# A four-layer graph network on one core: two sections of 64x64 products per pair, a tied norm in layer 3, and factors turned by chunks

## Chip, cores and metric

The kernel runs on one core of a Trainium2 chip, in one launch. The metric is the device time of that execution in microseconds (us). The host only lays the inputs out (the adjacency both ways round, some weights transposed).

The engines are named as in the profile: PE is TensorE (matrix products, with PEld its loading of the stationary operand), DVE is VectorE, ACT is ScalarE, POOL is GpSimd and SP is SyncE, which starts most transfers here. Each works through its own queue in order and waits for the others at semaphores.

## The reference

128 graphs of 64 nodes with 512 features, fp32, go through four layers. Every layer is `x = x + layer(relu(layernorm(x)), adj)`. Cut to what matters:

```python
# layer 0: a gate per node, softmax over the 64 nodes of a graph
q, k = split(h @ Wqk);  v = h @ Wv
agg = einsum('bij,bjd->bid', adj, k * mask)
w   = mask * einsum('bid,bid->bi', q, agg) / sqrt(512)
out = softmax(w, axis=1)[:, :, None] * v
# layer 1: one head, exp weights times adjacency
weight = adj * exp(einsum('bqd,bkd->bqk', h @ Wq.T + bq, h @ Wk.T + bk))
out = einsum('bqk,bkd->bqd', weight / weight.sum(2), h @ Wv.T + bv)
# layer 2: eight heads of 64, scores times adjacency, softmax, projection Wo
# layer 3: alpha = adj * exp(leaky_relu(sj + si + ab)), rows normalized to a transition
H = 0; Xk = h
for k in range(3):
    H = H + Xk @ Wk[k] + bk[k];  Xk = einsum('bij,bjd->bid', transition, Xk)
out = relu(H)
```

## The kernel before

**Blocks, pairs and steps.** A block is 256 tokens, that is four graphs, held as two tiles of 128 partitions (two graphs each). There are 32 blocks. Layers 0 and 1 run together, in pairs of blocks: for blocks 2p and 2p+1 the four steps are layer 0 of the even block, layer 0 of the odd one, layer 1 of the even one, layer 1 of the odd one (list `steps`). Their result goes to DRAM (`x1`); then layer 2 runs over all blocks, storing to `x2`, and layer 3 over all blocks.

**Products of 512x512.** The 256x512 by 512x512 products are made by a scheme of seven half-size products (class `Product`, L230). A product has two PSUM tiles, `ab_*` and `dc_*`, and runs as `first`, `second` and `late`; between them VectorE and ScalarE take intermediate values (`u_*`, L288, and `p_*`, L287 and L296) that free the accumulators for the late products. GpSimd forms four sums of the transposed input (`sums`, tiles S). The sums of the weights are formed once. `side_by_side` (L354) runs two products together and calls lists of `between` actions at three points: after the first product's `first`, and ahead of each `late`.

**Norms.** `norm` (L165) takes statistics on VectorE (`stats`, `mv`, `ve`), the root on GpSimd (`rstd`), a product on VectorE (`nmr`), and applies both with the relu on ScalarE (tiles `h`). `transposed` (L190) turns `h` on TensorE through PSUM tiles `tr`. `prepare(i + 1)` issues the next step's norm in the first `between` list of a step, `turned(i + 1)` its transposes in the last.

**Layer 0.** The neighbour sum `agg` is formed over `h` and multiplied by folded weights (Wq times Wk transposed: `fold`, slot `m0`), so that one product g and one product v are made per block. `am` is the adjacency times the mask column (GpSimd), `pa` (L400) the neighbour sums, one 64-wide product per graph into one half of a PSUM tile. ScalarE copies `pa` to `agg`; after the product g, VectorE makes the dots `w` and spreads them on a diagonal (`wd`). The rest (`layer0_end`, L572) runs in the next step's first `between` list: `sm_w` on TensorE, the softmax on VectorE and ScalarE, and x is updated.

**Layer 1.** Its products are again folded: g = h (Wq' Wk) and v. `products` (L378) makes the scores `sc` of a graph, 64 by 64 each, 32 matmuls with 128 rows by 64 columns of the array. `e` is their exp times the adjacency. `layer1_end` (L622) makes the row sums `den` and `po = e v`, one 64-wide product per graph; VectorE takes the reciprocals `r` (L636), adds `po r` to x (L638), and SyncE stores x.

**Where the 64-wide products stand.** All products that work on graphs (`sc`, `den`, `po`, `pa`) use parts of the array 64 wide; everything around them is 128 wide. `layer1_end` of block b is kept in `open_end`, which is called by the next step of an odd block. In a pair there are three places with such products: in the third step `sc` of the even block; in the fourth step the even block's end followed by `sc` of the odd block, after which the next pair's even `pa` comes; in the next pair's second step the odd block's end followed by that block's own `pa`. PSUM has eight banks: pool `ps_tr` two (transposes, `po`), `ps_mm` four (`ab_*` and `dc_*`, a `den` or `pa` at times), `ps_sc` two (scores, `pa`, row sums).

**Setup of layer 1.** `setup1` fetches Wq and Wk of layer 1, transposes both by `transpose_weights` (L419: sixteen 128x128 transposes per factor, into four PSUM tiles `tw_q` and four `tw_k`), and multiplies them in `folded` (`pf`, L450). The transposes go row chunk k by row chunk, each into every tile m. ScalarE copies all four `tw_q`; of the `tw_k` it copies those in `on_scalar`, VectorE the others, in the order of m.

**Layer 3.** For the first blocks, `layer3_norm` and `layer3_dots` run within layer 2's last steps. `layer3_dots` (L835) makes two dots per tile and the diagonal `di` (L848), from which TensorE makes `sm_i` (L408). A statement under `tc.issue_after(X)` is put behind instruction X in the order of issue; statements with no such tie are placed by a scheduler, which may put them ahead of what is written before them. A norm of layer 3 whose input has arrived can so stand earlier on VectorE than its place in the text.

Of the kernel before, what the change touches and what calls it, by code (L numbers as in the profile page):

```python
# [8 lines left out]
FP = mybir.dt.float32  # L9
# [4 lines left out]
P = 128  # L14
# [11 lines left out]
def kernel(ctx: ExitStack, tc: tile.TileContext, a: dict, out: bass.AP):  # L26
# [177 lines left out]
    def norm_T(x, name: str):  # L204
        hs = norm(x, name)
        return hs, transposed(hs, name)

    kept_ab, kept_p = [None], [None]
    behind = [None]

# [164 lines left out]
                act()  # L375
        return made

    def products(uT, vT, name: str):  # L378

        ps = ps_sc.tile([P, TT, N], FP, tag="sc", name=f"sc_{name}")  # L380
        for t in range(TT):
            for k in range(K):
                for g in range(2):
                    c = slice(t * P + g * N, t * P + (g + 1) * N)
                    nc.tensor.matmul(
                        ps[g * N : (g + 1) * N, t, :], uT[:, k, c], vT[:, k, c],
                        start=(k == 0), stop=(k == K - 1), skip_group_check=True,
                    )
        return ps
# [29 lines left out]
    def transpose_weights(*pairs):  # L419

        pts = [
            [
                pool.tile([P, K, P], FP, tag=tag, name=f"tw_{name}_{m}")
                for m, (pool, tag) in enumerate(places)
            ]
            for w, name, places, on_scalar, to in pairs
        ]
        for k in range(K):
            for (w, *_), mine in zip(pairs, pts):
                for m, pt in enumerate(mine):  # L430
                    nc.tensor.transpose(pt[:, k, :], w[k][:, m * P : (m + 1) * P], ident)
        last = [None, None]
        for m in range(K):
            for (_, _, _, on_scalar, to), mine in zip(pairs, pts):
                flat = mine[m].rearrange("p k i -> p (k i)")
                if m in on_scalar:
                    last[1] = nc.scalar.copy(to[m], flat)
                else:
                    last[0] = nc.vector.tensor_copy(to[m], flat)
        return last  # L440
# [29 lines left out]
    def setup1():  # L470


        qT, kT = (factor(a[f"L1_W{c}"], c, 1, nc.sync) for c in "qk")

        bias = big.tile([P, 2, P, K], FP, tag="v", name="b1qk")
        for i, n in enumerate(("L1_bq", "L1_bk")):
            nc.sync.dma_start(
                bias[:, i], a[n].rearrange("(o p) k -> o p k", o=1).to_broadcast([P, P, K])
            )
        w1v = fetched("L1_Wv", 3, nc.sync)  # L480
        yield

        rows = [med.tile([P, K, P], FP, tag="pT", name=f"b1_{i}", bufs=3) for i in range(2)]
        for i, r in enumerate(rows):
            nc.scalar.copy(r.rearrange("o k p -> o p k"), bias[:, i])
        rows = [r.rearrange("o k p -> o (k p)") for r in rows]
        yield
        u = const.tile([P, K], FP, tag="u1", name="u1")
        cc = small.tile([P, K], FP, tag="cc", name="c1", bufs=1)
        d = const.tile([P, 1], FP, tag="d1", name="d1")  # L490
        c1 = const.tile([P, 2, D + 1], FP, tag="u3", name="c1")[:, 0, :D]
        m = slot(2, "fold1")
        qt, kt = (
            f[K:] + [m[:, spare].rearrange("p k o -> p (k o)")]
            for f, spare in ((qT, T1), (kT, T2))
        )
        transpose_weights((qT, "q1", in_mm, range(K), qt))
        taken = transpose_weights((kT, "k1", elsewhere, (1, 3), kt))
        folded(kt, qt, 1, m, lambda: layer0_end(0, *softmax))
        formed(m, nc.gpsimd)  # L500
        with tc.issue_after(behind[0].ins):
            formed(w1v, nc.gpsimd)

        def dots(*sums):
            for to, x, by in sums:
                junk = med.tile([P, D], FP, tag="e2", name="bias1", bufs=3)
                nc.vector.scalar_tensor_tensor(
                    junk, x, 1.0, rows[by], ALU.mult, ALU.mult, accum_out=to
                )

        with tc.issue_after(taken[0].ins):
            dots((d, rows[0], 1))
            dots(*((u[:, k : k + 1], qT[k], 1) for k in range(K)))
            dots(*((cc[:, k : k + 1], kT[k], 0) for k in range(K)))

        crow = tc.dram_tile([1, D], FP, name="c1_row")
        nc.sync.dma_start(crow.rearrange("o (k p) -> p (o k)", p=P), cc)
        nc.sync.dma_start(c1, crow.to_broadcast([P, D]))
        w2 = [fetched(f"L2_W{c}", 4 + i, nc.sync) for i, c in enumerate("qk")]
        for w in w2:  # L520
            later(w)
        yield m, u, c1, d, w1v, w2


    def layer0(b: int, x, adjT, hs, hT, between, before):
        ops = sums(hT, f"0_{b}")
        gv = big.tile([P, 2, TT, D], FP, tag="qk", name=f"gv_{b}")
        am = small.tile([P, TT, N], FP, tag="am", name=f"am_{b}", bufs=2)
        with tc.issue_after(behind_norm[0][0].ins):
            nc.gpsimd.tensor_tensor(  # L530
# [2 lines left out]
                mcol[:, b * TT : (b + 1) * TT].unsqueeze(2).to_broadcast([P, TT, N]),  # L533
                ALU.mult,
            )
        before()
        pa = [
            pool.tile([P, D], FP, tag=tag, name=f"pa_{b}_{t}")
            for t, (pool, tag) in enumerate((
                ((ps_sc, "sc"), (ps_sc if b % 2 else ps_mm, "sc" if b % 2 else "mm"))  # L540
                if b else ((ps_tr, "tr"),) * 2
            ))
        ]
        aggs = [
            med.tile([P, D], FP, tag="agg", name=f"agg_{b}_{t}", bufs=2) for t in range(TT)
        ]
        for t, to, at in neighbour_sums(pa, am, hs):
            nc.scalar.copy(aggs[t][to], pa[t][at])

        parts = [  # L550
            (ops, m0, None, lambda p: p.store(gv[:, 0]), f"g0_{b}"),
# [43 lines left out]
    def layer1(b: int, x, adjT, hs, hT, between, before):  # L595
# [15 lines left out]
                    hc, hs[t], 1.0, c1, ALU.mult, ALU.mult, accum_out=be[:, t : t + 1]  # L611
                )
        nc.vector.tensor_scalar(be, be, d1, None, ALU.add)
        before()
        s = products(gT, hT, f"1_{b}")
        e = small.tile([P, TT, N], FP, tag="e", name=f"e1_{b}")
        for t in range(TT):
            nc.scalar.activation(e[:, t, :], s[:, t, :], AF.Exp, bias=be[:, t : t + 1])
        nc.vector.tensor_tensor(e, e, adjT, ALU.mult)
        return of_v, v, e  # L620

    def layer1_end(b: int, x, v, e, to):  # L622

        po = [ps_tr.tile([P, D], FP, tag="tr", name=f"po1_{b}_{t}") for t in range(TT)]
        pool, tag = (ps_mm, "mm") if b + 1 < n_blk else (ps_sc, "sc")
        den = [pool.tile([P, 1], FP, tag=tag, name=f"den1_{b}_{t}") for t in range(TT)]
        for t in range(TT):
            for g in range(2):
                nc.tensor.matmul(
# [5 lines left out]
        for t in range(TT):  # L635
            nc.vector.reciprocal(r[:, t : t + 1], den[t])  # L636
        for t, out_at, at in parts:
            nc.vector.scalar_tensor_tensor(  # L638
                x[out_at, t, :], po[t][at], r[at, t : t + 1], x[out_at, t, :], ALU.mult, ALU.add
            )  # L640
        nc.sync.dma_start(tokens(to), x)
# [189 lines left out]
    def layer3_norm(b: int):  # L831
        x, adjT = loaded3.pop(b)
        return x, adjT, norm(x, f"3_{b}")

    def layer3_dots(b: int, x, adjT, hs):  # L835


# [2 lines left out]
        for s in range(2):  # L840
# [4 lines left out]
                    accum_out=sij[:, s, t : t + 1],  # L845
                )
        di = small.tile([P, TT, N], FP, tag="e", name=f"di_{b}")
        nc.vector.tensor_tensor(  # L848
            di,
            eye.unsqueeze(1).to_broadcast([P, TT, N]),  # L850
            sij[:, 1, :].unsqueeze(2).to_broadcast([P, TT, N]),
# [128 lines left out]
    def prepare(i: int):  # L980
        layer, b = steps[i]
        if b not in loaded:
            loaded[b] = load_x(b, x_d[rows(b), :], 0), load_adjT(b, 0)
        normed[i] = norm(loaded[b][0], f"{layer}_{b}")

    def second():
        with tc.issue_after(of_m0.ins):
# [12 lines left out]
    def fetch2(b: int):  # L1000
        if b < n_blk:
            loaded2[b] = load_x(b, x1[b], 2), load_adjq(b)
# [28 lines left out]
    next(setup)  # L1031
    begun = []

    def nothing():
        pass

    open_end = nothing
    for i, (layer, b) in enumerate(steps):
        if i == len(steps) - 2:
            fetch2(0)  # L1040
# [7 lines left out]
            between[n].append(end)  # L1048
        begun = []
        if i + 1 < len(steps):  # L1050
            between[0].append(lambda: prepare(i + 1) if i else second())
            between[2].append(lambda: turned(i + 1))
        else:
            fetch2(1)
            between[0].append(lambda: first2(0, of_v))
            between[2].append(lambda: turned2(0))
        if layer == 0:
            softmax = layer0(b, *loaded[b], *normed[i], between, open_end if b % 2 else nothing)
            begun = [(0, lambda b=b, softmax=softmax: layer0_end(b, *softmax))]
        else:  # L1060
            of_v, *attention = layer1(
                b, *loaded[b], *normed[i], between, open_end if b % 2 else nothing
            )

            def open_end(b=b, a=attention):
                layer1_end(b, loaded[b][0], *a, x1[b])
                if b == n_blk - 2:
                    fetch2(2)

        if i == len(steps) - 3:  # L1070
            made2 = setup2()
# [7 lines left out]
    def layer3_step(b: int, ahead: bool = True):  # L1079
# [33 lines left out]
        yield  # L1113

    qk, ops = layer2_in(0, normed2[0], [
        [lambda: first2(1, of_v), chore], [open_end, chore], [lambda: turned2(1)]
    ])
    coming = values(0, ops)
    next(coming)
# [8 lines left out]
    for b in range(n_blk):  # L1128
# [44 lines left out]
            made3 = setup3()  # L1173
        if n_blk - 3 <= b < n_blk - 1:
            fetch3(b - n_blk + 3)
            normed3 = layer3_norm(b - n_blk + 3)
            with tc.issue_after(of_o.taken.ins):
                normed3 = layer3_dots(b - n_blk + 3, *normed3)
        elif b == n_blk - 1:
# [72 lines left out]
```

## Time and profile before

| what | value |
|---|---|
| median of 3 runs | 2629.41 us (2628.44 to 2629.85) |
| the profiled execution's own time | 2629.57 us |
| its span, first to last instruction | 2627.8 us |
| granted TensorE clock, mean | 0.999 |
| instructions in the span | 52810 |
| DMA | 129.81 MB, mean 49 GB/s |
| PE waiting for the first weights (`tw_q` for the transfer of q) | 4.9 us, 2 times |
| PE `pf` for DVE q and for ACT k | 0.6 us each, once |
| PE `ab_k` for DVE v, PE `ab_g` for DVE u_g | 0.2 us each, once |

The page of the profile gives for each engine the time in which it had an instruction at work, and its share of the span. The chain of waits follows the last instruction back to what released it, step by step. The waits view lists, for one engine, which semaphore ended its idle times: microseconds in total, number of times, and the longest. The timeline gives groups of like instructions in the order of their start: start, time from the first one's start to the last one's end, engine, line, operation, output and inputs, shape, and how many; in brackets, the idle time just before and what ended it. Matmuls are pipelined, so consecutive groups overlap by some 0.1 to 0.2 us, and the difference between two starts tells better than the length what a group cost.

### The profile page before, as it was taken

To read this page: it belongs to the slowest core of one execution; us is meant where nothing else is said; L and a number is where in the kernel's file an instruction comes from. 1 tells how busy PE (TensorE), PEld (TensorE's weight loads), DVE (VectorE), ACT (ScalarE), POOL (GpSimd) and SP (SyncE) were. 2 spreads that over 40 slices of the span, in tenths; PEclk is the share of its full clock that TensorE was granted. 3 is DMA by queue.
4 is the path that set the end of the run, shared out by engine and by line. 5 is a ranking of instruction groups with operands and counts; after the bars stand their busy time and mean duration, and the time that the engine had idled before them with its cause. 6 is when DMAs were issued, how large, how long until landed. Compare 5 with 4: busy or idle time off the path is not lost.

```text
span 2627.8 us, 52810 instructions
## 1 busy us (share of the span) xinstructions
PE 2612.6 (99%) x20752; PEld 2254.9 (86%) x20752; DVE 1705.0 (65%) x4400; ACT 953.5 (36%) x2294; POOL 1290.8 (49%) x1582
## 2 busy tenths in 40 slices
PE   9999999999999999999999999999999999999998
PEld 5888888888888889999999999999888888888876
DVE  5666666666666666566556656656677777777675
ACT  3333343333443333333333333333333333333332
POOL 3443433334334345656655655665565555555554
PEclk9999999999999999999999999999999999999999
DMA  5111111111111122111111111111211111111110
GB/s 172 65 35 35 35 36 35 44 44 35 43 43 35 35 67 79 46 45 40 45 47 39 38 54 38 39 46 45 74 51 52 52 52 52 52 52 52 52 43 33
DMA packets 103201, 129.81 MB, mean 49 GB/s; under 512 B 40870, under 2 KB 50086, under 8 KB 102952
## 3 DMA queue, kind: packets, MB, share of 16 engines
q1 hardware_dynamic: 102376, 125.38, 14.5%
q8 instruction: 164, 2.69, 0.4%
q10 hardware_dynamic: 576, 1.05, 0.1%
q14 instruction: 85, 0.70, 0.1%
HBM read 76.07 MB, written 50.34 MB: 48 GB/s over the span
## 4 chain that ended last, share of the span: by engine, by line
PE 97%; DVE 2%; DMA 0%; issue 0%; ACT 0%; POOL 0%; ACTq 0%; POOLq 0%; DVEq 0%
PE ab_y L258 13%; PE ab_v L258 13%; PE dc_y L258 9%; PE dc_v L258 9%; PE ab_g L251 4%; PE ab_k L251 4%; PE ab_q L251 4%; PE tr L196 4%; PE ab_o L258 4%; PE ab_g L258 4%; PE po L400 3%; PE dc_g L251 3%; PE dc_g L258 3%; PE dc_k L251 3%; PE dc_q L251 3%; PE dc_o L258 3%
## 5 line engine op out<-in xcount | busy, mean ns | idle before, releaser
L175 POOL TENSOR_TENSOR rstd<-ve,neghalf 128x2 f32<-128x2 f32 x128 | 89.7, 700 | 337.4 <-DVE ve L173 334.4
L185 ACT ACTIVATE h<-x,nmr,rstd 128x512 f32<-128x512 f32 x256 | 194.5, 806 | 165.9 <-DVE nmr L177 165.9
L258 PE MATMUL ab_y<-L_Wk,hT 128*128 128x256 f32 x768 | 203.9, 388 | 0.1
L258 PE MATMUL ab_v<-L_Wv,hT 128*128 128x256 f32 x768 | 200.7, 384 | 0.0
L258 PE MATMUL dc_v<-L_Wv,S 128*128 128x256 f32 x768 | 197.3, 379 | 0.0
L258 PE MATMUL ab_v<-L_Wv,S 128*128 128x256 f32 x768 | 197.1, 379 | 0.0
L258 PE MATMUL ab_y<-L_Wk,S 128*128 128x256 f32 x768 | 197.1, 379 | 0.0
L258 PEld LDWEIGHTS ab_y<-L_Wk,hT 128*128 128x128 f32 x768 | 138.0, 190 | 66.7 <-issue 24.3
L258 PE MATMUL dc_y<-L_Wk,S 128*128 128x256 f32 x768 | 192.7, 379 | 0.0
L945 POOL TENSOR_TENSOR tz<-tz,y 128x512 f32<-128x512 f32 x62 | 90.5, 1459 | 170.8 <-ACT tz L943 170.6
L170 DVE BATCH_NORM_STATS2 stats<-x 128x6 f32<-128x512 f32 x256 | 165.1, 676 | 0.1
L258 PEld LDWEIGHTS dc_y<-L_Wk,S 128*128 128x128 f32 x768 | 145.7, 190 | 20.5 <-issue 0.8
L258 PEld LDWEIGHTS ab_v<-L_Wv,S 128*128 128x128 f32 x768 | 145.9, 190 | 19.8
L258 PEld LDWEIGHTS ab_y<-L_Wk,S 128*128 128x128 f32 x768 | 145.9, 190 | 19.8
L258 PEld LDWEIGHTS dc_v<-L_Wv,S 128*128 128x128 f32 x768 | 143.4, 190 | 18.9 <-POOL L_Wv L87 0.8
L258 PEld LDWEIGHTS ab_v<-L_Wv,hT 128*128 128x128 f32 x768 | 135.9, 190 | 15.4
L196 PE MATMUL tr<-ident,h 128*128 128x128 f32 x1024 | 133.4, 273 | 0.0
L946 DVE SCALAR_TENSOR_TENSOR x<-tz,x 128x512 f32<-128x512 f32 x62 | 42.9, 693 | 129.6 <-POOL tz L945 129.6
L196 PEld LDWEIGHTS tr<-ident,h 128*128 128x128 f32 x1024 | 117.8, 141 | 7.8 <-issue 0.5
L223 POOL TENSOR_TENSOR S<-hT 128x256 f32<-128x256 f32 x128 | 100.2, 783 | 40.9 <-ACT hT L199 40.6
L226 POOL TENSOR_TENSOR S<-hT 128x256 f32<-128x256 f32 x128 | 106.9, 835 | 7.3 <-DVE hT L201 7.3
L224 POOL TENSOR_TENSOR S<-S,hT 128x256 f32<-128x256 f32 x128 | 102.3, 799 | 11.4 <-DVE ve L173 9.4
(255 smaller groups left out, 6409.7 us busy)
## 6 DMA issues: line engine op xcount, KB each, us to landing
x<-x SPq DMA_DIRECT2D x128, 512.0 KB, 3.5
x<-in_x_dram SPq DMA_DIRECT2D x32, 512.0 KB, 3.6
out_dram<-x SPq DMA_DIRECT2D x31, 512.0 KB, 2.8
adjT<-in_adjT_dram SPq DMA_DIRECT2D x64, 64.0 KB, 2.0
adjq<-in_adj_dram SPq DMA_DIRECT2D x64, 64.0 KB, 2.3
L_Wk<-in_L_Wk_dram SPq DMA_DIRECT2D x16, 256.0 KB, 4.7
L_Wv<-in_L_Wv_dram SPq DMA_DIRECT2D x12, 256.0 KB, 5.1
q<-in_L_Wqk_dram ACTq DMA_DIRECT2D x4, 256.0 KB, 4.7
```

The source lines that it names most:

```text
L170: nc.vector.bn_stats(stats[:, t, :], x[:, t, :])
L175: by_rows = nc.gpsimd.tensor_tensor(rstd, ve, neghalf, ALU.pow)
L185: nc.scalar.activation(h, x[:, t, :], AF.Relu, bias=nmr[:, t : t + 1], scale=rstd[:, t : t + 1])
L196: nc.tensor.transpose(pt[:, k, :], h[:, k * P : (k + 1) * P], ident)
L223: nc.gpsimd.tensor_tensor(S1, A21, A22, ALU.add)
L224: nc.gpsimd.tensor_tensor(S2, S1, A11, ALU.subtract)
L226: behind[0] = nc.gpsimd.tensor_tensor(S3, A11, A21, ALU.subtract)
L251: nc.tensor.matmul(dst[:, m * P : (m + 1) * P], w[:, place, k, m * P : (m + 1) * P], left[:, k, :], start=key not in self.begun, stop=last ...
L258: nc.tensor.matmul(dst, left[:, k, :], w[:, place, k, :], start=key not in self.begun, stop=last and k == 1, skip_group_check=True,)
L400: nc.tensor.matmul(ps[t][half[g ^ t]], e[half[g], t, :], us[t][half[g]], start=True, stop=True)
L945: nc.gpsimd.tensor_tensor(tz[t], tz[t], y0[:, t, :], ALU.add)
L946: nc.vector.scalar_tensor_tensor(x[:, t, :], tz[t], 0.0, x[:, t, :], ALU.max, ALU.add)
```

## The change

Three things are changed; the number of instructions of each kind stays as it was.

1. *Sections of 64-wide products in layers 0 and 1.* The neighbour sums of layer 0 become a function of their own (`layer0_sums`). In the fourth step of a pair, ahead of the odd block's scores, both neighbour sums of the next pair are made (`summed(b + 1)`, `summed(b + 2)`), then the even block's end, then `sc`. The odd block's end moves into the next pair's third step, ahead of the even block's `sc`. So the norm of the next pair's odd block is prepared within the fourth step too (`prepare(i + 2)` in its second `between` list). That odd block's `agg` takes buffers of the tag `pT`. The first column of `den` becomes a 129th column of the score tile in place of a PSUM tile of its own; its buffer in `ps_mm` goes to a `pa`. A norm of layer 0 that is prepared is tied behind the latest update of x in `layer1_end` (`added`).
2. *Layer 3.* The norms of layer 3 that are issued in layer 2's last steps are tied behind the latest `di` (`dotted`); the first one has no `di` before it and stays free.
3. *Layer 1's factors.* With one factor in a call, `transpose_weights` goes tile by tile: four transposes fill one PSUM tile, then the next. ScalarE copies `tw_k` 0 and 2 instead of 1 and 3.

```diff
@@ -207,2 +207,3 @@
 
+    added = [None]
     kept_ab, kept_p = [None], [None]
@@ -377,5 +378,4 @@
 
-    def products(uT, vT, name: str):
+    def products(uT, vT, ps):
 
-        ps = ps_sc.tile([P, TT, N], FP, tag="sc", name=f"sc_{name}")
         for t in range(TT):
@@ -427,6 +427,10 @@
         ]
-        for k in range(K):
-            for (w, *_), mine in zip(pairs, pts):
-                for m, pt in enumerate(mine):
-                    nc.tensor.transpose(pt[:, k, :], w[k][:, m * P : (m + 1) * P], ident)
+
+        if len(pairs) > 1:
+            turns = [(p, k, m) for k in range(K) for p in range(len(pairs)) for m in range(K)]
+        else:
+            turns = [(0, k, m) for m in range(K) for k in range(K)]
+        for p, k, m in turns:
+            w, pt = pairs[p][0], pts[p][m]
+            nc.tensor.transpose(pt[:, k, :], w[k][:, m * P : (m + 1) * P], ident)
         last = [None, None]
@@ -497,3 +501,3 @@
         transpose_weights((qT, "q1", in_mm, range(K), qt))
-        taken = transpose_weights((kT, "k1", elsewhere, (1, 3), kt))
+        taken = transpose_weights((kT, "k1", elsewhere, (0, 2), kt))
         folded(kt, qt, 1, m, lambda: layer0_end(0, *softmax))
@@ -524,5 +528,3 @@
 
-    def layer0(b: int, x, adjT, hs, hT, between, before):
-        ops = sums(hT, f"0_{b}")
-        gv = big.tile([P, 2, TT, D], FP, tag="qk", name=f"gv_{b}")
+    def layer0_sums(b: int, adjT, hs, pools):
         am = small.tile([P, TT, N], FP, tag="am", name=f"am_{b}", bufs=2)
@@ -535,12 +537,10 @@
             )
-        before()
+        tags = {ps_tr: "tr", ps_mm: "mm", ps_sc: "sc"}
         pa = [
-            pool.tile([P, D], FP, tag=tag, name=f"pa_{b}_{t}")
-            for t, (pool, tag) in enumerate((
-                ((ps_sc, "sc"), (ps_sc if b % 2 else ps_mm, "sc" if b % 2 else "mm"))
-                if b else ((ps_tr, "tr"),) * 2
-            ))
+            pool.tile([P, D], FP, tag=tags[pool], name=f"pa_{b}_{t}")
+            for t, pool in enumerate(pools)
         ]
+        tag, bufs = ("pT", 3) if b % 2 else ("agg", 2)
         aggs = [
-            med.tile([P, D], FP, tag="agg", name=f"agg_{b}_{t}", bufs=2) for t in range(TT)
+            med.tile([P, D], FP, tag=tag, name=f"agg_{b}_{t}", bufs=bufs) for t in range(TT)
         ]
@@ -548,2 +548,9 @@
             nc.scalar.copy(aggs[t][to], pa[t][at])
+        return aggs
+
+    def layer0(b: int, x, adjT, hs, hT, aggs, between):
+        ops = sums(hT, f"0_{b}")
+        gv = big.tile([P, 2, TT, D], FP, tag="qk", name=f"gv_{b}")
+        if aggs is None:
+            aggs = layer0_sums(b, adjT, hs, (ps_sc if b else ps_tr,) * 2)
 
@@ -613,4 +620,7 @@
         nc.vector.tensor_scalar(be, be, d1, None, ALU.add)
-        before()
-        s = products(gT, hT, f"1_{b}")
+        ps = ps_sc.tile([P, TT * N + 1], FP, tag="sc", name=f"sc_{b}")
+        for act in before:
+            act(ps[:, TT * N :])
+
+        s = products(gT, hT, ps[:, : TT * N].rearrange("p (t n) -> p t n", t=TT))
         e = small.tile([P, TT, N], FP, tag="e", name=f"e1_{b}")
@@ -621,7 +631,9 @@
 
-    def layer1_end(b: int, x, v, e, to):
+    def layer1_end(b: int, x, v, e, to, den=None):
 
         po = [ps_tr.tile([P, D], FP, tag="tr", name=f"po1_{b}_{t}") for t in range(TT)]
+        if den is None:
+            den = ps_sc.tile([P, 1], FP, tag="sc", name=f"den1_{b}_0")
         pool, tag = (ps_mm, "mm") if b + 1 < n_blk else (ps_sc, "sc")
-        den = [pool.tile([P, 1], FP, tag=tag, name=f"den1_{b}_{t}") for t in range(TT)]
+        den = den, pool.tile([P, 1], FP, tag=tag, name=f"den1_{b}_1")
         for t in range(TT):
@@ -637,3 +649,3 @@
         for t, out_at, at in parts:
-            nc.vector.scalar_tensor_tensor(
+            added[0] = nc.vector.scalar_tensor_tensor(
                 x[out_at, t, :], po[t][at], r[at, t : t + 1], x[out_at, t, :], ALU.mult, ALU.add
@@ -834,2 +846,4 @@
 
+    dotted = [None]
+
     def layer3_dots(b: int, x, adjT, hs):
@@ -847,3 +861,3 @@
         di = small.tile([P, TT, N], FP, tag="e", name=f"di_{b}")
-        nc.vector.tensor_tensor(
+        dotted[0] = nc.vector.tensor_tensor(
             di,
@@ -983,3 +997,6 @@
             loaded[b] = load_x(b, x_d[rows(b), :], 0), load_adjT(b, 0)
-        normed[i] = norm(loaded[b][0], f"{layer}_{b}")
+        with ExitStack() as behind_sums:
+            if added[0] and not layer:
+                behind_sums.enter_context(tc.issue_after(added[0].ins))
+            normed[i] = norm(loaded[b][0], f"{layer}_{b}")
 
@@ -1033,6 +1050,7 @@
 
-    def nothing():
-        pass
+    ends, aggs = {}, {}
+
+    def summed(b: int, hs, pools):
+        aggs[b] = layer0_sums(b, loaded[b][1], hs, pools)
 
-    open_end = nothing
     for i, (layer, b) in enumerate(steps):
@@ -1050,3 +1068,6 @@
         if i + 1 < len(steps):
-            between[0].append(lambda: prepare(i + 1) if i else second())
+            if i + 1 not in normed:
+                between[0].append(lambda: prepare(i + 1) if i else second())
+            if layer and b % 2:
+                between[1].append(lambda: prepare(i + 2))
             between[2].append(lambda: turned(i + 1))
@@ -1057,11 +1078,15 @@
         if layer == 0:
-            softmax = layer0(b, *loaded[b], *normed[i], between, open_end if b % 2 else nothing)
+            softmax = layer0(b, *loaded[b], *normed[i], aggs.pop(b, None), between)
             begun = [(0, lambda b=b, softmax=softmax: layer0_end(b, *softmax))]
         else:
-            of_v, *attention = layer1(
-                b, *loaded[b], *normed[i], between, open_end if b % 2 else nothing
-            )
+            before = []
+            if b % 2 and i + 2 < len(steps):
+                before.append(lambda _: summed(b + 1, normed[i + 1][0], (ps_sc, ps_mm)))
+                before.append(lambda _: summed(b + 2, normed[i + 2], (ps_mm, ps_mm)))
+            if b:
+                before.append(ends.pop(b - 1))
+            of_v, *attention = layer1(b, *loaded[b], *normed[i], between, before)
 
-            def open_end(b=b, a=attention):
-                layer1_end(b, loaded[b][0], *a, x1[b])
+            def ended(den=None, b=b, a=attention):
+                layer1_end(b, loaded[b][0], *a, x1[b], den)
                 if b == n_blk - 2:
@@ -1069,2 +1094,4 @@
 
+            ends[b] = ended
+
         if i == len(steps) - 3:
@@ -1115,3 +1142,3 @@
     qk, ops = layer2_in(0, normed2[0], [
-        [lambda: first2(1, of_v), chore], [open_end, chore], [lambda: turned2(1)]
+        [lambda: first2(1, of_v), chore], [ends[n_blk - 1], chore], [lambda: turned2(1)]
     ])
@@ -1175,3 +1202,6 @@
             fetch3(b - n_blk + 3)
-            normed3 = layer3_norm(b - n_blk + 3)
+            with ExitStack() as behind_dots:
+                if dotted[0]:
+                    behind_dots.enter_context(tc.issue_after(dotted[0].ins))
+                normed3 = layer3_norm(b - n_blk + 3)
             with tc.issue_after(of_o.taken.ins):
```

## The prediction

> **What bounds the kernel.** I read the page's busy shares and chain first, then TensorE's waits, then TensorE's timeline at the places that the diff touches.
>
> ```profile
> PE 2612.6 (99%) x20752; PEld 2254.9 (86%) x20752; DVE 1705.0 (65%) x4400; ACT 953.5 (36%) x2294; POOL 1290.8 (49%) x1582
> PE 97%; DVE 2%; DMA 0%; issue 0%; ACT 0%; POOL 0%; ACTq 0%; POOLq 0%; DVEq 0%
> ```
>
> TensorE is the bound from end to end. The change adds and removes no instruction on any engine (11,050 matmuls issued in both orders); it can gain only time in which TensorE stands still or changes its manner of work. The listed waits are short:
>
> ```profile
> PE ab_o L258 <- DVE u_o L288: 1.3, 1, 1.3
> ...
> PE sm_i L408 <- DVE di L848: 0.3, 1, 0.3
> ```
>
> Idle time after a wait is not all: a group that starts late costs more than its listed wait. So I price by differences of start times. In undisturbed stretches four 128x256 matmuls (one "piece") take 0.865 us from start to start, eight 128x128 ones 0.89. The sections of 64-wide products in layers 0 and 1 come three to a pair of blocks; these are the second and third (column 1 start, column 2 busy time):
>
> ```profile
> 220.17 1.03 PE L258 MATMUL dc_v<-L_Wv,S 128*128 128x256 f32 x4
> 221.13 0.29 PE L629 MATMUL den<-ones_bd,e 64*64 64x1 f32 x8
> 221.26 1.07 PE L400 MATMUL po<-v,e 64*64 64x512 f32 x8
> 222.26 1.15 PE L385 MATMUL sc<-hT,gT 128*64 128x64 f32 x32
> 223.34 1.09 PE L400 MATMUL pa<-h,am 64*64 64x512 f32 x8
> 224.36 1.13 PE L258 MATMUL dc_g<-fold,S 128*128 128x256 f32 x4
> 225.33 1.03 PE L258 MATMUL ab_g<-fold,hT 128*128 128x256 f32 x4
> ...
> 236.57 1.03 PE L258 MATMUL dc_v<-L_Wv,S 128*128 128x256 f32 x4
> 237.52 0.29 PE L629 MATMUL den<-ones_bd,e 64*64 64x1 f32 x8
> 237.66 1.07 PE L400 MATMUL po<-v,e 64*64 64x512 f32 x8
> 238.55 1.04 PE L400 MATMUL pa<-h,am 64*64 64x512 f32 x8
> 239.52 1.13 PE L258 MATMUL dc_g<-fold,S 128*128 128x256 f32 x4
> ```
>
> The reader is to see two things. The last 128-wide piece before a section takes 0.96 instead of 0.865, and the first one behind it 0.97. And po costs 0.89 before pa, which works the same 64x64 quarters, but 1.00 before sc, which works in 128x64; pa before a 128-wide piece costs 0.97 to 1.02.
>
> **Change 1: three sections become two.** Now, per pair (period 59.66 us), with 0.095 entering and 0.10 leaving each:
> - A = sc of the even block: 0.095+1.08+0.10 = 1.275.
> - B = den and po, sc, pa: 0.095+0.13+1.00+1.08+1.02+0.105 = 3.43.
> - C = den and po, pa: (0.96-0.865)+0.14+0.89+0.97+0.105 = 2.19, with rounding.
>
> Together 6.895. After: A' = den and po of the odd block before, then sc: 0.095+0.13+1.00+1.08+0.10 = 2.405. B' = both pa of the next pair, den and po of the even block, sc: 0.095+0.89+0.89+0.13+1.00+1.08+0.10 = 4.185. Together 6.59: 0.305 less for each of 15 pairs (the first A' has no end, the last B' no pa) is **4.6 us**. A pa priced at 0.97 in B' would take back 0.08x2x15 = 2.4; I take 0.89, because in B' another 64x64 product stands behind each pa, as pa stands behind po in C.
>
> The Trainium skill, "TensorEngine Tiling (Array Packing)", Key Properties, says that changing the tiling mode drains TensorE, while another tile of one mode does not. By it the eight changes of mode per pair become six; the third section's two cost 2.19-0.14-0.89-0.89 = 0.27, so the gain would be 0.27x15 = 4.1 rather than 4.6, and the trace agrees in kind (po 1.00 against 0.89).
>
> What the moves put at risk, and what covers it:
> - den's first column is now a column of the score tile, so sc waits until VectorE has taken its reciprocal. In A', den is done some 0.2 after the section's start S, the reciprocal (0.11 each, two in 0.22) needs a free VectorE and ends about S+1.1; sc would start at S+1.225. Cover 0.1; I take 0. If it fails by 0.1 each time: 1.6. In B' sc comes at S+3.0, the reciprocal by S+2.3.
> - B' takes all four buffers of the product pool (three pa, one den). ScalarE copies three pa tiles in 1.77; the next dc_g needs the fourth at B'+3.54, and starts at 4.08.
> - The odd block's end moves into A', between two norms on VectorE: x is updated by A'+1.2, its norm now issues behind that update, statistics (676 ns each, four) and ScalarE's four relus follow to A'+8.2, then u_v at A'+8.65; TensorE goes on at A'+9.1, and needs the buffer at A'+10.6. Cover 1.5.
> - SyncE: the store of x (512 KB, 3.5 us) now stands in A' ahead of the next adjacency, which lands about A'+4.5; pa reads it at A'+14.2. GpSimd's am, behind the odd block's rstd at about A'+6, is as early.
>
> All these I cost at nothing.
>
> **Change 2: the first pair.** In the fourth step of the first pair ab_g starts 1.23 after the piece before it, 0.1 more after: VectorE's three updates x<-po (2.28 us from 120.38) delay the softmax of layer 0 and with it u_g at 126.83. They leave this step. Gain 0.37+0.1, taken **0.45** (0 if another load fills the place).
>
> **Change 3: layer 1's factors by chunks.** Now every PSUM tile is complete only with the last of 16 transposes:
>
> ```profile
> 40.74 2.07 PE L431 MATMUL tw_q<-ident,q 128*128 128x128 f32 x16
> 42.65 1.91 PE L431 MATMUL tw_k<-ident,k 128*128 128x128 f32 x16
> 45.14 2.81 PE L450 MATMUL pf<-q,k 128*128 128x512 f32 x6 [0.58 <-ACT k L437]
> ```
>
> 32 transposes at the trace's 0.87 per eight (tr rows) are 3.48: pf could start at 44.22, 0.92 earlier. By chunks, the first copy starts after four transposes; copies of k on two engines end at about 43.7, 44.9, 44.5, 45.5, and pf needs them at 44.2, 45.1, 45.95, 46.8. Gain **0.9** (0 if each copy waits for its neighbour).
>
> **Change 4: layer 3's second norm behind the dots of the first.** Now this norm floats into layer 2's last but one step. Its VectorE rows (nmr waits 0.80 for GpSimd) push u_o back:
>
> ```profile
> 1877.24 0.68 DVE L177 SCALAR_TENSOR_TENSOR nmr<-mv,rstd 128x2 f32<-128x2 f32 x1 [0.80 <-POOL rstd L175]
> ...
> 1883.02 0.41 DVE L288 TENSOR_TENSOR u_o<-ab_o,p_o 128x256 f32<-128x256 f32 x1
> ...
> 1883.48 1.13 PE L258 MATMUL ab_o<-L_Wo,cT 128*128 128x256 f32 x4 [1.29 <-DVE u_o L288]
> ```
>
> Undisturbed this ab_o would start at 1881.73; it starts 1.75 late, and restarts with 0.1: 1.85 to be gained. But the norm then stands behind di (end D): u_q 0.34, two statistics and their ends to ve at D+1.82, rstd 0.7 on GpSimd, nmr to D+2.79, the first relu on ScalarE to D+3.70; p_k's copy is behind it on ScalarE, D+4.10 with u_k on VectorE behind that, and TensorE's second ab_k could start at D+4.56, where it is wanted at about D+3.25. That gives back 1.3+0.1. Net gain **0.45**, between 1.85 (nothing queues) and -0.5 (the relus of both halves come ahead of p_k).
>
> ```profile
> 92.62 1.51 ACT L185 ACTIVATE h<-x,nmr,rstd 128x512 f32<-128x512 f32 x2
> 94.03 0.36 ACT L287 COPY p_g<-ab_g 128x256 f32<-128x256 f32 x1
> ```
>
> Here too a copy whose matmuls had ended near 91 starts only when the relus are through. The Trainium skill ("TensorE: Matmul & The Clock Gate", the section on the array of 32x32 parts) calls ScalarE's and VectorE's queues strict first-in first-out; it speaks against this edit, and were it untrue the sum would be 1.4 larger.
>
> **Sum.** 4.6+0.45+0.9+0.45 = 6.4 of the profiled execution's 2629.57 (span 2627.8 and 1.77 around it): 2623.2. That execution lies 0.16 above the median of the runs, 2629.41; so I forecast **2623.1**.
>
> **Rivals.**
> 1. *The wait takes the place of what it saves.* sc waits for the reciprocal 0.1 in each A' (1.6 back), and layer 3 gives its gain back and 0.5 more (0.95): 2623.1+1.6+0.95 = 2625.7, within the bound. For it: 0.1 of cover is little beside VectorE rows of 0.4 to 0.7 that may stand ahead. Against: at A' VectorE has just stored v and waits. Chance 0.14.
> 2. *Sections cost nothing, only modes do, and pa costs its 0.97 everywhere:* 4.6-2.4 = 2.2 from sections, and 0 from layer 3: 2629.41-2.2-0.9-0.45 = 2625.9. Against: C's po at 0.89. Chance 0.05.
> 3. *Slower: the odd step's in-order queues.* In A' the norms of two blocks queue behind the update of x, and p_v's copy behind their relus. If the four statistics doubled in length while GpSimd works beside them (layer 0's dot goes from 0.74 to 1.20 in such places), they would be 2.4 late, less the cover of 1.5: 0.9 x 15 = 13.5 given back, less the forecast's gain: 2623.1+13.5 = 2636.6. It is slower than before once the chain is 1.9 late in every pair. For it: this is the longest chain that the change builds. Against: statistics take 676 ns on the mean of all 256, and GpSimd is idle between rstd and the next sums. Chance 0.09, and 0.04 for a like overrun elsewhere (the four-buffer pool).
>
> **Chances and range.** The forecast has 0.68. 0.2% is 5.26 us, about what measurements of this kernel can tell from no change: faster is below 2624.15, slower above 2634.7. Rivals 1 and 2 fall within (0.19), rival 3 and its like above (0.13). The most that the terms allow is 4.6+0.92+0.47+1.85 = 7.84, and the runs before lie up to 0.9 below their median: 2629.41-7.84-0.9 = 2620.7. The least is near nothing; at 2628.2 the range holds both small rivals with their ends, and leaves out the slower cases and some 0.05.
>
> **What would show it.** One 64x64 section less per pair: po and pa at 0.89 within sections, sc last; no wait of sc for the reciprocal in the list; the period of a pair at 59.35 instead of 59.66. pf of layer 1 starting 0.9 earlier after tw_q; no wait of pf. ab_g of the fourth step without its 0.20. No wait of ab_o for u_o, but one of about 1 us of ab_k for u_k. A new row "PE sc <- DVE r" would show rival 1, "PE ab_v <- DVE u_v" thirty or fifteen times rival 3; with pa at 0.97 and the period unmoved, the price of a section was wrong.

## The result, and the profile after

The changed kernel takes 2621.18 us (median of 7 runs, 2620.54 to 2622.81), the kernel before 2629.41 (7 runs, 2628.44 to 2630.48): 8.2 us less, a ratio of 0.997 with a 95% interval of 0.996 to 0.998. The forecast was 2623.1, its range 2620.7 to 2628.2. The profiled execution took 2621.18, with a span of 2619.3.

The head of the changed kernel's page and the chain of waits:

```profile
PE 2605.9 (99%) x20752; PEld 2258.2 (86%) x20752; DVE 1709.4 (65%) x4400; ACT 952.1 (36%) x2294; POOL 1290.7 (49%) x1582
PE 97%; DVE 2%; DMA 0%; issue 0%; ACT 0%; POOL 0%; POOLq 0%; ACTq 0%; DVEq 0%
```

The same instructions, and TensorE still the bound. What it waited for (us in total, times, longest), without the first weights:

```profile
PE ab_k L252 <- DVE u_k L289: 1.2, 1, 1.2
PE pf L454 <- DVE q L443: 0.6, 1, 0.6
PE ab_o L259 <- DVE u_o L289: 0.6, 1, 0.6
PE sm_i L408 <- DVE di L862: 0.3, 1, 0.3
...
PE sc L385 <- DVE r L648: 0.2, 1, 0.2
```

ab_k's wait for u_k is new, ab_o's has become shorter but stays, sc waits once for the reciprocal, and one wait of pf and the one of ab_g are gone. Apart from the moved sections, TensorE's order of work is the same, so the difference of the two spans, 8.5, can be divided by the start times of six of its instructions ("last matmul" is the last group of four, `dc_y`; the two stretches left out differ by less than 0.05):

| stretch of TensorE's timeline | before | after | difference | in the forecast |
|---|---|---|---|---|
| start of the span to the first `pf` | 11.85 | 11.48 | -0.37 | - |
| layer 1's first `tw_q` to its first `pf` | 4.40 | 3.49 | -0.91 | -0.9 |
| first `sc` to layer 2's first scores | 930.47 | 924.28 | -6.19 | -4.6-0.45 |
| those to the last matmul | 1602.43 | 1602.87 | +0.44 | -0.45 |
| last matmul's start to the end of the span | 8.07 | 6.59 | -1.48 | - |

In the timeline of TensorE (start, time, line, operation, how many), a pair's two sections now look like this (`...` stands for lines left out):

```profile
202.05 1.03 PE L259 MATMUL dc_v<-L_Wv,S 128*128 128x256 f32 x4
...
203.14 1.07 PE L400 MATMUL po<-v,e 64*64 64x512 f32 x8
204.14 1.15 PE L385 MATMUL sc<-hT,gT 128*64 128x64 f32 x32
205.22 1.16 PE L252 MATMUL dc_g<-S,fold 128*128 128x128 f32 x8
206.22 1.06 PE L252 MATMUL ab_g<-hT,fold 128*128 128x128 f32 x8
...
217.63 1.03 PE L259 MATMUL dc_v<-L_Wv,S 128*128 128x256 f32 x4
218.59 1.95 PE L400 MATMUL pa<-h,am 64*64 64x512 f32 x16
...
220.44 1.07 PE L400 MATMUL po<-v,e 64*64 64x512 f32 x8
221.44 1.15 PE L385 MATMUL sc<-hT,gT 128*64 128x64 f32 x32
222.52 1.13 PE L259 MATMUL dc_g<-fold,S 128*128 128x256 f32 x4
223.49 1.03 PE L259 MATMUL ab_g<-fold,hT 128*128 128x256 f32 x4
```

The first is 2.42 long (den starts at 203.00, 0.085 late; 206.22 is 0.11 late), where 2.405 was reckoned; the second 4.13, where 4.185 was: both pa take 1.77, and den 0.08 behind them. The three sections of before took 6.895, these 6.55. The factors, by chunks:

```profile
40.38 1.91 PE L435 MATMUL tw_q<-ident,q 128*128 128x128 f32 x16
42.12 1.91 PE L435 MATMUL tw_k<-ident,k 128*128 128x128 f32 x16
43.87 2.81 PE L454 MATMUL pf<-q,k 128*128 128x512 f32 x6
```

No idle time stands ahead of pf any more; 43.87-40.38 = 3.49. And layer 3's first two norms, on all engines, in the order of time (the brackets give the idle time before, and what ended it):

```profile
1867.72 0.16 DVE L177 SCALAR_TENSOR_TENSOR nmr<-mv,rstd 128x2 f32<-128x2 f32 x1 [0.80 <-POOL rstd L175]
...
1874.99 1.13 PE L259 MATMUL ab_o<-L_Wo,cT 128*128 128x256 f32 x4 [0.56 <-DVE u_o L289]
...
1888.06 0.81 ACT L185 ACTIVATE h<-x,nmr,rstd 128x512 f32<-128x512 f32 x1 [5.90 <-DVE nmr L177]
1888.78 0.35 ACT L288 COPY p_k<-ab_k 128x256 f32<-128x256 f32 x1
...
1889.16 0.42 DVE L289 TENSOR_TENSOR u_k<-ab_k,p_k 128x256 f32<-128x256 f32 x1 [1.14 <-ACT p_k L288]
...
1889.64 1.16 PE L252 MATMUL ab_k<-hT,L_Wk 128*128 128x128 f32 x8 [1.21 <-DVE u_k L289]
```

From the relu to TensorE this is the chain that the prediction wrote down, with 1.21 where it had 1.3. But ab_o still waits, and some way ahead of it stands an nmr that waits 0.80 for GpSimd: that is the norm of layer 3's *first* block, which the change leaves free.

### The profile page after: what moved, and what is told of

The parts are those of the page before. It is cut to its first block, busy times and chain, and to the rows that moved or that the text cites. A ratio compares the mean times of both kernels' runs of the same rounds, so it can differ in the third digit from the quotient of the medians.

```text
span 2619.3 us, 52774 instructions
## 1 busy us (share of the span) xinstructions
PE 2605.9 (99%) x20752; PEld 2258.2 (86%) x20752; DVE 1709.4 (65%) x4400; ACT 952.1 (36%) x2294; POOL 1290.7 (49%) x1582
## 4 chain that ended last, share of the span: by engine, by line
PE 97%; DVE 2%; DMA 0%; issue 0%; ACT 0%; POOL 0%; POOLq 0%; ACTq 0%; DVEq 0%
PE ab_y L259 13%; PE ab_v L259 12%; PE dc_y L259 9%; PE dc_v L259 9%; PE ab_k L252 4%; PE ab_g L252 4%; PE ab_o L259 4%; PE tr L196 4%; PE ab_q L252 4%; PE ab_g L259 4%; PE po L400 3%; PE dc_g L252 3%; PE dc_g L259 3%; PE dc_k L252 3%; PE dc_q L252 3%; PE dc_o L259 3%
## 5 line engine op out<-in xcount | busy, mean ns | idle before, releaser
L288 ACT COPY p_y<-ab_y 128x256 f32<-128x256 f32 x96 | 35.7, 372 | 190.5 <-PE ab_y L259 190.5
```

Of the source, the lines that this page charges most:

```text
L288: kept_p[0] = nc.scalar.copy(self.p1, self.a)
```

## The experiments

**The factors alone.**

```diff
+            turns = [(0, k, m) for m in range(K) for k in range(K)]
...
-        taken = transpose_weights((kT, "k1", elsewhere, (1, 3), kt))
+        taken = transpose_weights((kT, "k1", elsewhere, (0, 2), kt))
```

> The kernel before with the chunk-wise transposes of layer 1's factors alone. As priced: pf follows the first tw_q by 3.5 us instead of 4.4, everything behind it 0.9 earlier, about 2628.5 us. Rival (the copies were hidden anyway, pf waits for the next copy instead): 2629.4, with a wait of pf further on. A second question is the tail: from the last matmul's start to the end of the span it was 8.07 us in the kernel before and 6.60 in the changed one, with the same instructions in it. If the tail hangs on the length of the program, this one (as many instructions as before) keeps about 8.1; if it differs from execution to execution, it may be anything from 6.6 to 8.1.

2628.45 against 2628.98 us (ratio 0.9996, interval 0.9988 to 1.0005): too little to tell from no change by the time alone. The trace tells it: pf at 43.66, tw_q at 40.17, so 3.49 apart as in the changed kernel, no wait of pf in layer 1, and no new one. The tail was 8.04.

**The tie alone, and the change without it.**

```diff
-            normed3 = layer3_norm(b - n_blk + 3)
+            with ExitStack() as behind_dots:
+                if dotted[0]:
+                    behind_dots.enter_context(tc.issue_after(dotted[0].ins))
+                normed3 = layer3_norm(b - n_blk + 3)
```

> The kernel before with layer 3's second norm tied behind di, alone. By the two traces: the wait of ab_o for u_o shrinks by 1.0 and a wait of ab_k for u_k of 1.2 (1.5 with its restart) comes, so 0.4 slower, 2629.8 us. By the prediction's term (ab_o's stall goes whole, 1.85, and 1.4 comes back): 2629.0, without a wait of ab_o.

> The changed kernel without the tie of layer 3's second norm. By the traces it should be 0.4 faster than the changed kernel, 2620.7 us, with ab_o waiting 1.3 for u_o and no wait of ab_k for u_k. By the prediction's term the tie gains 0.45, and this one stands at 2621.6.

The tie alone: 2628.47 against 2628.98 (ratio 0.9999, 0.999 to 1.0007), no slower by its time. Its trace has both waits as expected, 0.6 for u_o and 1.2 for u_k, but also a tail of 6.98 instead of 8.07, which hides the 0.4. Without the tie, 2620.81 (2620.47 to 2621.28), where 2620.7 was expected and the prediction's term gave 2621.6; ab_o waits 1.3 again and ab_k for u_k not at all. The kernel before stood at 2628.98 beside these runs and at 2629.41 beside the changed kernel's, so the times alone do not settle 0.4. The traces do: from layer 2's first scores to the last matmul the run without the tie took 1602.46, the changed kernel 1602.87, and the kernel before 1602.43. The tie costs 0.4 where it stands.

**The tie one place later.**

```diff
-                    behind_dots.enter_context(tc.issue_after(dotted[0].ins))
+                    behind_qk.enter_context(tc.issue_after(of_qk[b + 1][1].taken.ins))
```

> The changed kernel with the same norm tied one place later, behind the last store of layer 2's q and k of the last block, where the steps before have a norm of layer 2 and the last has none. If the wait of ab_k for u_k comes from p_k standing behind the norm's relu on ScalarE, it goes whole: 1.5 faster than the changed kernel, 2619.7 us, ab_o's 0.56 remaining. Rival (the norm only delays the next thing, u_v of the last block's values): 2621.2, with a wait of ab_v for u_v of about 1 us.

2619.79 us (2619.43 to 2620.27), and 1601.41 from layer 2's first scores to the last matmul: 1.46 less than the changed kernel, where 1.5 was expected. u_k now follows u_q at once, and TensorE, too:

```profile
1885.20 0.41 DVE L289 TENSOR_TENSOR u_k<-ab_k,p_k 128x256 f32<-128x256 f32 x1
...
1888.12 1.06 PE L252 MATMUL ab_k<-hT,L_Wk 128*128 128x128 f32 x8
```

ab_k does not wait for u_k, nor ab_v for u_v. So ab_k's wait did come from p_k standing behind a relu on ScalarE, as forecast, and an idle place was some 7 us further on (1892.04 instead of 1885.36 for its statistics).

**What is left of ab_o's wait.** In the kernel of the last experiment one instruction on VectorE changes its place; `held` is given for layer 3's first block alone, and is the addition that makes cT.

```diff
+        with ExitStack() as behind_ctx:
+            if held:
+                behind_ctx.enter_context(tc.issue_after(held.ins))
             scaled = nc.vector.scalar_tensor_tensor(
                 nmr, mv[:, :, 0], -1.0, rstd, ALU.mult, ALU.mult
```

> The kernel of tie_later with one instruction moved on VectorE: nmr of layer 3's first norm, which waits 0.80 for GpSimd's rstd, stands behind the addition that makes cT instead of ahead of it. If what is left of ab_o's wait (0.56, 0.7 with its restart) comes from that wait at the head of VectorE's queue, cT and all behind it start 0.7 earlier and the wait goes: 2619.1 us. Rival (the two subtractions e-mx, which take 1.1 and 1.2 instead of 0.65 beside GpSimd's sums, set u_o's time wherever they start): ab_o still waits 0.3 to 0.6, 2619.5 to 2619.8.

2619.1 us (2619.01 to 2619.89), a ratio of 0.9963 (0.9949 to 0.9977) to the kernel before, and 1600.71 from layer 2's first scores to the last matmul: 0.7 less than the run before it. From its timeline:

```profile
1866.90 0.68 DVE L784 TENSOR_TENSOR cT<-pc,b2v 128x512 f32<-128x512 f32 x1
...
1867.79 0.16 DVE L182 SCALAR_TENSOR_TENSOR nmr<-mv,rstd 128x2 f32<-128x2 f32 x1 [0.21 <-POOL rstd L177]
...
1870.26 2.13 DVE L730 TENSOR_TENSOR e<-e,mx 128x512 f32<-128x512 f32 x2
...
1873.91 0.41 DVE L294 TENSOR_TENSOR u_o<-ab_o,p_o 128x256 f32<-128x256 f32 x1
...
1874.59 1.03 PE L264 MATMUL ab_o<-L_Wo,cT 128*128 128x256 f32 x4
```

The wait for rstd is 0.21 in place of 0.80. Counted from the scores of block 30 (1866.21 here, 1866.14 in the changed kernel), u_o starts after 7.70 in place of 8.38, and ab_o follows the piece before it (1873.72) by 0.87, without a wait. The rival's rows are there too: the two e-mx take 2.13, nearly the 2.22 of the changed kernel. So u_o's time does not hang on them alone: it moves with nmr's place.

**The sections alone.** The changed kernel with the two other parts undone.

```diff
-        turns = [(0, k, m) for m in range(K) for k in range(K)]
...
-        taken = transpose_weights((kT, "k1", elsewhere, (0, 2), kt))
+        taken = transpose_weights((kT, "k1", elsewhere, (1, 3), kt))
...
-                behind_dots.enter_context(tc.issue_after(dotted[0].ins))
```

> The kernel before with the moved sections alone (layer 1's factors and layer 3's norm as before). From the traces: 0.40 less for each pair behind the first, 0.3 back in the last pair for the reciprocal, 0.4 from the first pair's stall: 6.1 less until layer 2's first scores. By the prediction's terms 4.6+0.45 = 5.05. So TensorE's last matmul 6.1 (or 5.05) earlier against the kernel before, apart from what the first weights' arrival makes; in time about 2622.5 to 2623.

2621.51 against 2629.59 us (ratio 0.997, 0.9959 to 0.9982). In the trace, first sc to layer 2's scores took 924.29, 6.2 less than before: the terms of the traces hold, those of the prediction (5.05) are 1.1 short. The time is 1 below the 2622.5 to 2623 that was expected, because the tail is 6.61 here too; it comes with the sections.

**A change of mode within a section.**

```diff
+        last = before[-1:] if b % 2 else []
+        for act in before[: len(before) - len(last)]:
             act(ps[:, TT * N :])
         s = products(gT, hT, ps[:, : TT * N].rearrange("p (t n) -> p t n", t=TT))
+        for act in last:
+            act(ps[:, TT * N :])
```

> The changed kernel, in whose fourth step the order inside the section is both pa, sc, den and po instead of both pa, den and po, sc: as many sections, but one more change between 64x64 and 128x64 products per pair. By rows (pa before sc 1.00 for 0.885, den 0.13 for 0.08, po last about 1.00): 0.16 a pair, 2.5 in all, 2623.7. By drains alone at 0.135 a change: 2.0, 2623.2. If only entering and leaving the 128-wide work cost something: 2621.2.

2623.62 us (2622.65 to 2624.2), 2.4 above the changed kernel. The section, in the timeline:

```profile
218.74 1.95 PE L400 MATMUL pa<-h,am 64*64 64x512 f32 x16
220.62 1.15 PE L385 MATMUL sc<-hT,gT 128*64 128x64 f32 x32
...
221.84 1.07 PE L400 MATMUL po<-v,e 64*64 64x512 f32 x8
222.83 0.92 PE L259 MATMUL dc_g<-fold,S 128*128 128x256 f32 x3
```

Both pa before sc take 1.88 (1.77 before den), den 0.14 (0.08), po 0.99 (1.00): 0.16 more a pair, 926.73-924.28 = 2.45 in all. So it is not only entering and leaving the 128-wide work that costs, but a change of the array's division within a section too. That agrees with what the Trainium skill says in "TensorEngine Tiling (Array Packing)", Key Properties, of the drain at a change of mode; it gives no figure for it.

**Layer 0's norms untied.** The tie behind the update of x is a part of the change that the prediction used only in passing.

```diff
-            if added[0] and not layer:
-                behind_sums.enter_context(tc.issue_after(added[0].ins))
```

> The changed kernel without the tie of layer 0's norms behind the update of x: four statistics now stand ahead of the reciprocal on VectorE in the third step. If sc really waits for that reciprocal with a cover of 0.1 to 0.2, each third step loses what VectorE has in front of it beyond its idle time: 1 to 2.5 us a pair, 15 to 37 in all, 2636 to 2658, with sc for r in the list of waits 14 or 15 times. Rival (the column in the score tile does not hold sc back): 2621, and an unchanged list.

2674.71 us (4 runs, 2667.19 to 2680.53; ratio to before 1.0171, 1.0156 to 1.0187): slower by more than the whole range that was expected. Its waits, and its timeline where the third step of the second pair begins its section:

```profile
PE sc L385 <- DVE r L648: 34.0, 15, 2.9
```

```profile
210.12 0.67 DVE L177 SCALAR_TENSOR_TENSOR nmr<-mv,rstd 128x2 f32<-128x2 f32 x1 [1.87 <-POOL rstd L175]
210.72 0.15 DVE L648 RECIPROCAL r<-sc 128x1 f32<-128x1 f32 x1
...
210.93 1.97 PE L385 MATMUL sc<-hT,gT 128*64 128x64 f32 x32 [2.38 <-DVE r L648]
```

sc does wait for the reciprocal, and this stands behind an nmr that waits 1.87 for GpSimd. That makes 34.0. But from the first sc to layer 2's scores it is 977.77-924.28 = 53.5. The rest is in the clock that was granted (window; length, busy time of PE, PEld, DVE, ACT and POOL with the number of instructions; then PEclk, the granted share of TensorE's clock):

```profile
208.00:210.00 2.00, 0.55 (x8) 0.00 (x0) 0.25 (x1) 0.00 (x0) 2.00 (x4) 1.00 0.00 0
210.00:212.00 2.00, 1.07 (x20) 1.07 (x22) 1.88 (x6) 1.17 (x2) 0.78 (x2) 0.58 0.00 0
212.00:214.00 2.00, 2.00 (x23) 1.88 (x20) 1.92 (x6) 0.87 (x3) 0.00 (x0) 0.50 0.00 0
214.00:216.00 2.00, 2.00 (x12) 2.00 (x11) 0.44 (x3) 0.85 (x2) 0.70 (x1) 0.50 0.62 222
216.00:218.00 2.00, 2.00 (x15) 2.00 (x15) 0.00 (x0) 0.76 (x2) 0.40 (x1) 0.72 0.31 80
```

sc takes 1.97 where it took 1.15, and the pieces behind it are slow until about 217. Over the run, a mean granted clock of 0.992 is 0.008 of 2672 us, some 21, short of full; 53.5-34.0 is 19.5. The four runs had 0.992, 0.995, 0.990 and 0.992; with this shortfall taken off, each comes to 2653 or 2654, within the range that was expected. So the waits were priced rightly and the clock was not foreseen.

**Both kernels once more.** Nothing is edited.

> The kernel before, unchanged, profiled once more. If the tail behind the last matmul (8.07 us there, 8.04 and 6.98 in two variants of it, 6.5 to 6.6 in three of the changed kernel) belongs to the program, it is 8.0 to 8.1 again; if it differs from execution to execution, anywhere from 6.5 to 8.1. The same for the start of the first pf: 11.85 before, 11.0 to 11.5 in the others.

> The changed kernel, unchanged, profiled once more: the tail behind the last matmul 6.5 to 6.7 as in the four other kernels with the moved sections, if it belongs to the program; up to 8.1 if it differs from execution to execution.

The tails were 8.0 (2626.7-2618.70) and 6.6 (2619.2-2612.59), so they belong to the program. The first pf started at 10.72 and 11.40, against 11.85 and 11.48: that differs from execution to execution.

## Why the prediction was right, and where it was not

- **What bounds the kernel** and that only stalls and changes of mode could be gained: right; TensorE does the same work in both.
- **Sections**, 4.6: right in mechanism, too small. The period of a pair fell from 59.66 to 59.26, 0.40 in place of 0.305. The second section is 0.055 shorter than reckoned (den takes 0.08 behind pa, not the 0.13 that it took behind a 128-wide piece: a change of mode was charged twice), the first 0.015 longer, and 0.04 are the transposes of the third step, which take 0.88 from start to start now and took 0.92 before; 0.015 is not traced. Fifteen times 0.40 is 6.0; the last pair gives 0.3 back. pa at 0.885 decided against the bound of 2.4.
- **The reciprocal**, taken at nothing with a cover of 0.1: right, and this cover is thin. In the timeline of VectorE after the change:

```profile
203.52 0.41 DVE L314 TENSOR_TENSOR v<-dc_v,u_v 128x256 f32<-128x256 f32 x1
203.85 0.16 DVE L648 RECIPROCAL r<-sc 128x1 f32<-128x1 f32 x1
```

It ends at 204.01, and sc starts at 204.14. Only in the last pair, where the next norm is one of layer 2 and has no tie, statistics stand ahead and sc waits 0.18. The run with layer 0's norms untied showed that the mechanism of rival 1's first half is real, and that it would have decided; what rules it out is the tie behind the update of x.
- **The four buffers, ScalarE's order and SyncE's transfers**, costed at nothing: no wait appears for any of them.
- **The first pair**, 0.45: 0.41. Second to third sc took 44.55 and 42.02, against 44.08 and 41.96 in the next pair, so the excess fell from 0.47 to 0.06.
- **The factors**, 0.9: 0.91.
- **Layer 3**, 0.45 gained: wrong in sign, 0.44 lost. The failed step is "1.85 to be gained": it put all of ab_o's delay on the second norm's rows and took it that everything behind them would move up as far. These are rows of VectorE's timeline, before and after:

```profile
1875.34 0.67 DVE L767 TENSOR_TENSOR cT<-pc,b2v 128x512 f32<-128x512 f32 x1
1875.93 0.15 DVE L177 SCALAR_TENSOR_TENSOR nmr<-mv,rstd 128x2 f32<-128x2 f32 x1
...
1877.84 1.28 DVE L703 TENSOR_TENSOR e<-s,adjq 128x512 f32<-128x512 f32 x2
...
1880.22 1.28 DVE L713 TENSOR_TENSOR e<-e,mx 128x512 f32<-128x512 f32 x2
```

```profile
1867.80 0.68 DVE L779 TENSOR_TENSOR cT<-pc,b2v 128x512 f32<-128x512 f32 x1
1868.40 1.28 DVE L715 TENSOR_TENSOR e<-s,adjq 128x512 f32<-128x512 f32 x2
...
1870.78 2.22 DVE L725 TENSOR_TENSOR e<-e,mx 128x512 f32<-128x512 f32 x2
```

From the scores of block 30 (1873.60 and 1866.14), the first `e` came after 4.24 and comes after 2.26, 1.98 earlier. But u_o came after 9.42 and comes after 8.38, only 1.04 earlier: the two e-mx, which took 1.20 from start to next start in their late place, now take 2.15, beside GpSimd's sums (in the step before, block 29's, they took 2.1 in both kernels). And the first norm's nmr, which stood behind cT without a wait, now waits its 0.80 ahead of it. So ab_o gained 1.03 (9.88 to 8.85 from the scores), and 0.7 of wait and restart is left. What comes back was forecast at 1.4 and measured 1.47. The tie one place later takes the 1.47 away, and the one instruction moved takes the 0.7, so that both are shown; that the sums lengthen the e-mx is read from the rows alone. The loss came near the prediction's bound of -0.5 without its reason: one relu stands ahead of p_k, not both.
- **What no term held:** 1.48 in the tail and 0.37 ahead of the first pf. The first is of the program, as the repeated profiles show, the second of the execution. Without the tail the median would be near 2622.7, so that the sum of 6.4 owes its closeness there to errors of both signs: the sections and the first pair gave 1.1 more than forecast, layer 3 gave 0.9 less. That closeness is in part luck.
- **Rivals.** The second half of rival 1 came true, layer 3 giving back 0.89 (0.95 there), and its first half did not. Rivals 2 and 3 did not occur: the period moved and pa cost 0.885; no wait of ab_v for u_v exists.
- **Slips that change no reading.** No page has 11,050 matmuls; both count 20752. The sum gives 2623.0 rather than 2623.1, and in rival 3 four statistics of 676 ns doubled would be 2.7 late, not 2.4.

## What to carry to other kernels

Price a regrouping of small products by the changes of the array's division that it removes, read from start to start, and not by the listed waits; and charge each change once. When a delayed instruction has two causes on its engine, take away both on paper before the whole delay is put on one: look for every instruction in the queue that itself waits, and for what the rows that move up will now run beside. A tie on the order of issue is priced by what it is put in front of; an empty slot of the same kind in a neighbouring step is the first place to try.

## What the runs showed of the hardware

- **A stall can cost more than its length.** After waits of 2.4 to 2.9 us the granted clock fell to 0.50 in the run with layer 0's norms untied, for some 3 to 7 us, but not after every one. Of the fourteen sc behind such a wait, five took 1.97 at once; behind five more the clock fell within 2 us (sc started at 338.64, and the clock was 0.50 from 341 to 343); behind four it stayed at 1.00. Over the run, 34.0 of waiting cost 53.5, and the mean granted clock was 0.992 instead of 1.000. The waits of 1.2 and 1.3 in the other kernels had no such effect. The Trainium skill, "TensorE: Matmul & The Clock Gate", Part 1, tells of a clock that is halved by a free-running window of activity, which agrees with a fall after some of equal waits; it speaks of an idle window of some 3.4 us, and here 2.4 were enough.
- **Rows of VectorE and GpSimd lengthen where they meet.** In the timeline of the run with nmr moved, the two e-mx take 2.13 together beside these sums, which take 0.73 alone:

```profile
1870.66 1.18 POOL L230 TENSOR_TENSOR S_c<-S_c,cT 128x256 f32<-128x256 f32 x1
1871.92 1.07 POOL L231 TENSOR_TENSOR S_c<-cT,S_c 128x256 f32<-128x256 f32 x1
```

In the kernel before, the sums were over by 1880.08 and the e-mx that began at 1880.22 took 1.28. The nmr of 0.68 that the prediction shows is another such row: it began at 1877.24, beside a sum that ran from 1877.16 to 1877.89, and the nmr at 1875.93 took 0.15. The Trainium skill's "SBUF — State Buffer", in the part on who interferes with whom, calls the ports that the two share an exclusive lock, for which the second comer waits until the first has finished; the lengths agree. No run here took the overlap away by itself.
- **The end of a program has a price of its own.** The tail was 8.0 to 8.1 in three profiles with 85 packets on the queue of instructions named q14, 6.98 in one with 84, 6.5 to 6.6 in those with 83; three of the 85 fall into the last 28 us of the kernel before, none there in the changed one. The work itself is the same: from the last group of matmuls to the issue of the last two stores it is 2.73 in both kernels. The difference lies behind it, and a part of it in these stores, which took 2.6 to land (median) and take 2.1. That the packets cause the longer tail was not tried.
